# Keys and values of a second attention projected during the first attention instead of inside the second

## The chip, the core and the metric

The kernel runs on one core of a Trainium2 chip. The metric is the time of one execution on the device in microseconds. The core's engines work side by side, each through a queue of its own and in order: TensorE (PE, matrix products; its weight loads are shown apart as PEld), VectorE (DVE), ScalarE (ACT), GpSimd (POOL) and SyncE (SP, which here only issues DMA transfers). They wait for each other through semaphores. PE writes its products to PSUM, in banks that DVE or ACT empty; POOL works on SBUF alone.

## The reference

Two decoder layers run over 16 batches of 128 tokens with 256 features. With all that does not bear on the change left out, the reference is:

```python
x = x + tanh(g_xattn[0]) * L0_xattn(layernorm(x), ctx, ...)   # self- and cross-attention
x = x + tanh(g_ffn[0])   * L0_ffn(layernorm(x), ...)          # gated feed-forward
x = x + tanh(g_xattn[1]) * L1_xattn(layernorm(x), ctx, ctx, mask, ...)
x = x + tanh(g_ffn[1])   * L1_ffn(layernorm(x), ...)          # 8 experts, one per token

# L1_xattn: 32 query heads in 8 groups of 4, head size 8, causal and padded
q = (Q @ w_q.T).reshape(B, S, G, HG, HD)
k = (K @ w_k.T).reshape(B, S, G, HD)      # K = V = ctx
v = (V @ w_v.T).reshape(B, S, G, HD)
scores = einsum('bnghd,bmgd->bnghm', q, k) / sqrt(HD)
attn = softmax(where(causal & not_padded, scores, -inf))
out = einsum('bnghm,bmgd->bnghd', attn, v).reshape(B, S, D) @ w_o.T + b_o
```

The keys and values of the second attention (L1_xattn) depend on the context `ctx` and two weight matrices alone. They do not depend on `x`, so they can be computed at any time.

## The kernel before

The kernel has four stages. **The first attention** is a loop over 32 units of four steps each: units 0 to 15 are self-attention, one batch each, and units 16 to 31 cross-attention, one batch each. One loop index `n` (lines 651 to 690) drives a pipeline in which at every step different units are at different stages: `do(n, lag, name)` runs a stage for the unit and quarter that are `lag` steps behind. A step holds a score product (L503), maximum and exponentials, transposes of the probabilities (L539), the value product (L549), the output product (L590), and for a later unit two projections of 512 columns (L422), their eviction by ACT (L434) and the transposes of the normalized heads (L485, evicted by ACT at L494). The output product of a unit's last eight heads needs `cat`, which POOL writes at the end of a quantizing chain (L237). Projections go through two PSUM banks with the tag `mm`. A self-attention unit's residual is stored to DRAM (`x1`, L609) and its scaled input too (`xqx`, L400), all on SP's queue, as are the loads of `xb` (L587), of `ctx` for the cross units (L346, a tag with two buffers) and of the weights.

**The feed-forward** follows (L721 to L757), group by group of four batches.

**The second attention** is a loop of 64 steps, four to a batch (L1132 to L1160), over four groups of four batches. For a group, `front_step` loads the context transposed (`cT`, 512 KB, issued by POOL at L933) and the mask, normalizes `x`, transposes it, and projects queries and keys (`qk`, two column blocks each, L982, evicted by ACT at L987 and L989). The key weights come in with every group's eight columns repeated four times, once for each query head of the group, so a key projection has 256 columns. For a batch, `keys` makes `kb` on POOL, the keys masked by head (L1000), projects the values (L1006) and has DVE copy them four times into a zero-padded tile `vpad` (L1011). A step then does mask (L1022) and score products (L1029), the maximum on DVE, exponentials on ACT (L1045), transposes (L1056), DVE copies (L1057), and every second step the value products (L1072). A batch's output product is at L1085. The first group's front runs inside the feed-forward, at `g == 1`.

**The experts** close the kernel; they read rows that POOL scattered to DRAM (L870).

Functions issue their instructions in the order of the source, but the build may put a queue in another order: it places an instruction when its inputs and its buffer are free, and prefers the one that is earlier in the source.

Of the kernel before, what the change touches and what calls it, by code (L numbers as in the profile page):

```python
# [9 lines left out]
F32 = mybir.dt.float32  # L10
# [4 lines left out]
AF = mybir.ActivationFunctionType  # L15
# [3 lines left out]
P = 128  # L19
B = 16  # L20
DM = 256
KD = DM // P
# [13 lines left out]
def flamingo_kernel(  # L36
# [27 lines left out]
    nc = tc.nc  # L64
# [4 lines left out]
    NH, NG, HD = 32, 8, 8  # L69
# [4 lines left out]
    psum = psum0.enter_context(tc.tile_pool(name="psum", bufs=2, space=bass.MemoryType.PSUM))  # L74
    dram = ctx.enter_context(tc.tile_pool(name="dram", bufs=1, space=bass.MemoryType.DRAM))
# [4 lines left out]
    def ps_mm(shape):  # L80
        return ps("mm", shape, 2)
# [30 lines left out]
    def kpn(ap):  # L112
        return ap.rearrange("(k p) n -> p k n", p=P)
# [129 lines left out]

    xqx = dram.tile([B, P, KD * P], F32, name="xqx")
    x1 = dram.tile([B, P, DM], F32, name="x1")
    NU = 2 * B


# [2 lines left out]
    with (  # L251
# [359 lines left out]
        units = [Unit(u) for u in range(NU)]  # L611


        loads = {}

        def at(n, f, *args):
# [151 lines left out]
    SCALE1 = 1.0 / math.sqrt(HD)  # L768
    NQ = NH // NG
# [9 lines left out]
    for j in range(B):  # L779
# [9 lines left out]
        out=before, in_=ones, pattern=[[1, P]], compare_op=ALU.is_gt, fill=0.0,  # L789
# [20 lines left out]
    def route(b0, G):  # L810
# [73 lines left out]
    cq = f1.enter_context(tc.tile_pool(name="a1c", bufs=1, side="right", reuse_waits="tile"))  # L884
    gp = f1.enter_context(tc.tile_pool(name="a1f", bufs=2, side="right", reuse_waits="tile"))
    aq = cq.tile([P, KD, DM], F32, name="aq")
    ak = cq.tile([P, KD, DM], F32, name="ak")
    av = cq.tile([P, KD, NG * HD], F32, name="av")
    ao = cq.tile([P, KD, DM], F32, name="ao")
    bo = cq.tile([P, DM], F32, name="bo")  # L890
    nc.sync.dma_start(out=aq, in_=kpn(aqT))
    nc.sync.dma_start(out=ak, in_=kpn(akT))
    nc.sync.dma_start(out=av, in_=kpn(avT))
    nc.sync.dma_start(out=ao, in_=kpn(aoT))
    nc.sync.dma_start(out=bo, in_=b_o.partition_broadcast(P))

# [6 lines left out]
        out=causal, in_=causal, pattern=[[-1, P]], compare_op=ALU.is_ge, fill=NEG,  # L903
# [5 lines left out]
    for q in range(P // 32):  # L909
        rows = hmask[32 * q : 32 * q + 32, :]  # L910
        nc.gpsimd.memset(rows, 1.0)
        nc.gpsimd.affine_select(
            out=rows, in_=rows, pattern=[[-HD, NQ]], compare_op=ALU.is_ge, fill=0.0,
# [3 lines left out]
            out=rows, in_=rows, pattern=[[HD, NQ]], compare_op=ALU.is_ge, fill=0.0,  # L917
# [4 lines left out]
    vpads = [cq.tile([P, NG, NQ, 32], F32, name=f"vpad{i}") for i in range(2)]  # L922
# [6 lines left out]
    front = {}  # L929

    def load(g):
        cT = gp.tile([P, KD, NT], F32, tag="cT", name="cT")
        nc.gpsimd.dma_start(out=cT, in_=kpn(ctxT)[:, :, g * NT : (g + 1) * NT])  # L933
        mi = gp.tile([P, NT], I32, tag="mi", name="mi", bufs=1)
        nc.sync.dma_start(
            out=mi, in_=mask[g * NT : (g + 1) * NT].partition_broadcast(P)
        )
        comb = gp.tile([P, G, P], BF16, tag="comb", name="comb")
        pad = gp.tile([P, NT], F32, tag="pad", name="pad", bufs=1)
        nc.vector.tensor_scalar(pad, mi, 0.0, NEG, ALU.is_equal, ALU.mult)  # L940
# [4 lines left out]
        front[g] = {"cT": cT, "comb": comb}  # L945

    def norm(g):
        rows = [x[b] for b in range(g * G, (g + 1) * G)]
# [22 lines left out]
            nc.scalar.copy(hT[:, k, :], pt.rearrange("p n t -> p (n t)"))  # L971
        front[g]["hT"] = hT

    def qk(g, i, c):

        f = front[g]
        if c == 0:
            f[i] = gp.tile([P, KD, NT], F32, tag="qk"[i], name="qk"[i] + "T")
        w, src = ((aq, f["hT"]), (ak, f["cT"]))[i]
        pm = psum.tile([P, NT], F32, tag="mm", name="ps_mm")  # L980
        for k in range(KD):
            nc.tensor.matmul(  # L982
                pm, w[:, k, c * P : (c + 1) * P], src[:, k, :],
                start=(k == 0), stop=(k == KD - 1),
            )
        if i == 0:
            nc.scalar.activation(f[i][:, c, :], pm, AF.Copy, scale=SCALE1)  # L987
        else:
            nc.scalar.copy(f[i][:, c, :], pm)  # L989

    kbs, vps, es, eTs, oTs, scs, mxs = {}, {}, {}, {}, {}, {}, {}

    def keys(b):

        g, j = divmod(b, G)
        f = front[g]
        tok = slice(j * P, (j + 1) * P)
        kb = ap.tile([P, KD, NQ, P], F32, tag="kb", name="kb")
        for c in range(KD):
            nc.gpsimd.tensor_tensor(  # L1000
                kb[:, c], f[1][:, c, None, tok].to_broadcast([P, NQ, P]),
                hmask[:, :, None].to_broadcast([P, NQ, P]), ALU.mult,
            )
        pm = psum.tile([P, NG, HD], F32, tag="mm", name="ps_mm")
        for k in range(KD):
            nc.tensor.matmul(  # L1006
                pm, f["cT"][:, k, tok], av[:, k, :], start=(k == 0), stop=(k == KD - 1)
            )
# [3 lines left out]
        kbs[b], vps[b] = kb, vp  # L1012

    def scores(n):

        b, c, p = n // 4, n // 2 % 2, n % 2
        g, j = divmod(b, G)
        f = front[g]
        tok = slice(j * P, (j + 1) * P)
        s = psum.tile([P, 2, NQ, P], F32, tag="sc", name="ps_sc", bufs=2)  # L1020
        for i in range(2):
            nc.tensor.matmul(  # L1022
                s[:, i], identb, f["comb"][:, j, None, :].to_broadcast([P, NQ, P]),
                start=True, stop=False,
            )
        with tc.high_priority(offset=100):
            for i in range(2):
                rows = slice(32 * (2 * p + i), 32 * (2 * p + i) + 32)
                nc.tensor.matmul(  # L1029
                    s[:, i], f[0][rows, c, tok], kbs[b][rows, c], start=False, stop=True  # L1030
                )
        scs[n] = s

# [64 lines left out]
    def front_step(g, i):  # L1098

        if i == 0:  # L1100
            load(g)
            norm(g)
        elif i == 3:
            turn(g)
        elif 5 <= i < 9:
            qk(g, (i - 5) // 2, (i - 5) % 2)

    hds = {}
    for g in range(B // G):
# [3 lines left out]
        for b in range(g * G, (g + 1) * G):  # L1113
# [18 lines left out]
    for n in range(-2, N1 + 5):  # L1132
# [17 lines left out]
        g, i = divmod(n + 12, 16)  # L1150
# [10 lines left out]
    for stages in routes:  # L1161
        for _ in stages:
# [13 lines left out]
    for e in range(NE):  # L1176
# [6 lines left out]
            out=xe, in_=disp[e * CAP : (e + 1) * CAP, :].rearrange("(c p) d -> p c d", p=P)  # L1183
# [14 lines left out]
        for c in range(NCC):  # L1198
            po = ps_sc([P, DM])
            for f in range(NFC):  # L1200
# [9 lines left out]
                out=out_rows,  # L1210
# [81 lines left out]
```

## Time and profile before

| what | time |
|---|---|
| three runs, median (lowest to highest) | 1516.2 us (1514.5 to 1518.29) |
| the profiled execution, its own time | 1515.79 us |
| its span | 1514.1 us |
| PE busy | 1381.9 us (91% of the span) |
| PE weight loads busy | 1004.0 us (66%) |
| DVE busy | 1022.1 us (68%) |
| ACT busy | 810.6 us (54%) |
| POOL busy | 672.7 us (44%) |
| TensorE clock granted, mean | 0.974 of full |

Times of the profile are microseconds from the start of the span, unless marked ns. A line such as `L1006 PE MATMUL ps_mm<-av,cT 128*128 128x64 f32 x4` names the source line, the engine, the operation, the tile written and the tiles read, the shape, and how many such records follow each other. A float32 product of this kernel leaves two records, so x4 are two matmul instructions. A bracket gives the idle time before a group and what ended it. Ends of matmuls are modelled, starts are recorded.

### The profile page before, as it was taken

The numbers are of one execution on the slowest core, as the hardware profiler recorded it, in microseconds if no ns is written. First come the engines' busy times: TensorE is split into PE (matmuls) and PEld (weight loads), VectorE is DVE, ScalarE is ACT, GpSimd is POOL, SyncE is SP. The second block draws the span as 40 slices with busy tenths as digits, with TensorE's granted clock in tenths as the row PEclk, the third lists the DMA queues.
The fourth block names the chain that finished last, engine by engine and source line by source line (L and its number), as shares of the span: only waits on it lengthen the run. The fifth ranks groups of instructions, "written<-read, shape, count | busy, mean of one in ns | idle before, by whom it ended". The sixth has DMA issues, their size and how long they took to land. (4 is left out here: it accounts for less than half of the span.)

```text
span 1514.1 us, 24690 instructions
## 1 busy us (share of the span) xinstructions
PE 1381.9 (91%) x8612; PEld 1004.0 (66%) x8612; DVE 1022.1 (68%) x2756; ACT 810.6 (54%) x2421; POOL 672.7 (44%) x574
## 2 busy tenths in 40 slices
PE   2789899898988999999999987999999999996998
PEld 1477677677766777777777764555556565654887
DVE  8988878786887876767777664533678787882100
ACT  3666666666666766666666651543445454542121
POOL 4577676777667455565655553120121311111111
PEclk9799999999999999999999998999999999996999
DMA  4301001000031100000000006200300100012662
GB/s 120 118 8 32 15 15 32 11 19 15 22 91 50 49 26 11 18 15 18 15 15 19 5 8 194 61 0 0 112 22 8 50 9 36 9 40 66 202 195 64
DMA packets 51116, 68.69 MB, mean 45 GB/s; under 512 B 5291, under 2 KB 37739, under 8 KB 50992
## 3 DMA queue, kind: packets, MB, share of 16 engines
q1 hardware_dynamic: 36912, 41.31, 9.0%
q10 hardware_dynamic: 11456, 17.63, 3.6%
q0 software_dynamic: 2624, 8.16, 1.5%
q8 instruction: 69, 1.13, 0.3%
q14 instruction: 55, 0.45, 0.1%
HBM read 50.53 MB, written 16.81 MB: 44 GB/s over the span
## 5 line engine op out<-in xcount | busy, mean ns | idle before, releaser
L531 POOL TENSOR_TENSOR e<-e,sums 128x512 f32<-128x512 f32 x128 | 139.7, 1091 | 226.7 <-DVE sums L527 108.8
L474 POOL TENSOR_TENSOR raw<-raw,q_r 128x512 f32<-128x512 f32 x192 | 211.9, 1129 | 19.8 <-DVE q_r L464 18.9
L519 ACT ACTIVATE e<-ps_sc,mx 128x128 f32<-128x128 f32 x512 | 181.4, 369 | 65.0 <-DVE mx L511 56.5
L443 DVE BATCH_NORM_STATS2 q_st<-raw 128x6 f32<-128x128 f32 x768 | 174.0, 278 | 61.7 <-ACT raw L434 61.3
L1045 ACT ACTIVATE e<-ps_sc,mx 128x128 f32<-128x128 f32 x512 | 139.7, 383 | 117.5 <-DVE mx L1036 106.4
L590 PE MATMUL ps_acc<-wp,cat 128*128 128x512 f32 x512 | 159.4, 433 | 27.4 <-POOL cat L237 26.9
L237 POOL TENSOR_TENSOR cat<-e_t,e_e 128x1024 fp32r<-128x1024 bf16 x64 | 136.3, 2129 | 47.4 <-DVE e_t L231 47.4
L541 ACT COPY eT<-ps_tr 128x512 f32<-128x512 f32 x128 | 75.4, 589 | 151.7 <-PE ps_tr L539 151.6
L503 PE MATMUL ps_sc<-kT,qT 128*128 128x128 f32 x1024 | 140.4, 280 | 17.1 <-ACT qT L494 17.1
L503 PEld LDWEIGHTS ps_sc<-kT,qT 128*128 128x128 f32 x1024 | 131.0, 193 | 35.4 <-ACT qT L494 28.7
L1000 POOL TENSOR_TENSOR kb<-kT,hmask 128x512 f32<-128x512 f32 x32 | 33.6, 1068 | 243.8 <-PE ps_sc L1029 184.5
L590 PEld LDWEIGHTS ps_acc<-wp,cat 128*128 128x128 f32 x512 | 94.7, 191 | 69.6 <-POOL cat L237 35.9
L549 PE MATMUL ps_pv<-eT,vt 128*128 128x256 f32 x512 | 132.8, 381 | 1.0 <-DVE cat_y L560 1.0
L485 PE MATMUL ps_tr<-ident,raw 128*128 128x128 f32 x768 | 115.4, 277 | 16.1 <-POOL raw L474 14.2
L434 ACT COPY raw<-ps_mm 128x512 f32<-128x512 f32 x192 | 114.0, 594 | 26.6 <-PE ps_mm L422 24.1
L485 PEld LDWEIGHTS ps_tr<-ident,raw 128*128 128x128 f32 x768 | 91.9, 142 | 50.4 <-POOL raw L474 23.5
L549 PEld LDWEIGHTS ps_pv<-eT,vt 128*128 128x128 f32 x512 | 96.5, 190 | 31.5 <-issue 11.4
L560 DVE TENSOR_TENSOR cat_y<-ps_pv,r_sm 128x512 bf16<-128x512 f32 x128 | 86.9, 679 | 39.9 <-PE ps_pv L549 39.7
L511 DVE TENSOR_REDUCE mx<-ps_sc 128x4 f32<-128x512 f32 x128 | 87.1, 680 | 36.5 <-PE ps_sc L503 35.9
L494 ACT ACTIVATE qT<-ps_tr,hv 128x512 f32<-128x512 f32 x128 | 101.1, 790 | 17.5 <-PE ps_tr L485 15.5
L519 ACT ACTIVATION_READ_ACCUMULATOR e<-ps_sc,mx 128x1 f32 x512 | 105.7, 206 | 0.0
L1036 DVE TENSOR_REDUCE mx<-ps_sc 128x8 f32<-128x1024 f32 x64 | 78.1, 1221 | 25.6 <-PE ps_sc L1029 23.5
(227 smaller groups left out, 2769.0 us busy)
## 6 DMA issues: line engine op xcount, KB each, us to landing
w1t<-in_w ACTq DMA_DIRECT2D x8, 1024.0 KB, 5.1
w2t<-in_w ACTq DMA_DIRECT2D x8, 1024.0 KB, 5.5
disp<-empty SPq DMA_DIRECT2D x16, 257.0 KB, 8.3
xe<-disp SPq DMA_DIRECT2D x8, 514.0 KB, 3.6
stage<-in_wprojT SPq DMA_DIRECT2D x16, 256.0 KB, 2.8
xg<-in_x SPq DMA_DIRECT2D x4, 512.0 KB, 3.9
xb<-in_x SPq DMA_DIRECT2D x16, 128.0 KB, 2.0
ctx<-in_ctxT SPq DMA_DIRECT2D x16, 128.0 KB, 2.2
```

The costliest lines, as they stand in the source:

```text
L237: ins = nc.gpsimd.tensor_tensor(dst, t[:, part], e[:, part], ALU.subtract)
L434: nc.scalar.copy(raw.rearrange("p h d -> p (h d)"), pm)
L443: nc.vector.bn_stats(self.st[:, 4 * blk + j, :], self.raws[blk][:, j, :])
L474: ins = nc.gpsimd.tensor_tensor(src, src, self.r[:, 4 * blk : 4 * blk + 4, None].to_broadcast([P, 4, P]), ALU.mult,)
L485: nc.tensor.transpose(pt[:, j, :], src[:, j, :], ident)
L494: nc.scalar.activation(dst, pt, AF.Identity, scale=hv[:, col : col + 1], bias=hv[:, col + 1 : col + 2])
L503: nc.tensor.matmul(pscore[:, j, :], qT[:, j, :], self.kT[:, 2 * c + j // 2, :], start=True, stop=True,)
L519: nc.scalar.activation(e[:, j, :], pscore[:, j, :], AF.Exp, bias=self.mx[:, j : j + 1], accum_out=sums[:, j : j + 1],)
L531: nc.gpsimd.tensor_tensor(e, e, sums[:, :, None].to_broadcast([P, 4, P]), ALU.mult)
L549: nc.tensor.matmul(pv[:, 2 * g : 2 * g + 2, :], self.vt[:, gg * P : (gg + 1) * P], eT[:, 2 * g : 2 * g + 2, :], start=True, stop=True,)
L590: nc.tensor.matmul(self.acc, self.cat[c // 2][:, h % 8, :], wpr[self.cross, c][:, j, :, :], start=(h == 0), stop=(h == 15),)
L1045: nc.scalar.activation(e[:, i, :], s[:, i // NQ, i % NQ, :], AF.Exp, bias=mx[:, i : i + 1])
```

## The change

The keys and values of the second attention are computed during the first attention's self-attention units, one batch at a time, and kept in two DRAM tensors, `k1s` (64 rows, one for each group and feature, by all tokens) and `v1s` (tokens by 64). In step `n = 4b + 3` batch `b` is projected, for `b` up to 14, and batch 15 at `n = 61`; the call stands between the step's second projection and its output product. Each takes two matmuls for the keys, two for the values, two ACT copies and two stores on SP. The batch's context is loaded four steps ahead, into the tag `ctx` that the cross units use. The key weights are loaded without the fourfold repetition.

The second attention loses its key projections, value projections, the load of `cT`, and two weight loads. It loads instead, on SP, for each group the keys by 16 transfers of eight partitions (each repeats a group's keys for the query heads) and the values by one. The padded values are now written by one POOL copy per batch in place of four DVE copies.

```diff
@@ first attention @@
+    k1s = dram.tile([NG * HD, B * P], F32, name="k1s")
+    v1s = dram.tile([B * P, NG * HD], F32, name="v1s")
...
+        ak = ap.tile([P, KD, NG * HD], F32, tag="ak", name="ak", bufs=1)
+        av = ap.tile([P, KD, NG * HD], F32, tag="av", name="av", bufs=1)
+        cxs = {}
+
+        kv1_at = {4 * b + 3: b for b in range(B - 1)}
+        kv1_at[4 * (B - 1) + 1] = B - 1
+
+        def load_kv1(b):
+            if b == 0:
+                for k in range(KD):
+                    nc.sync.dma_start(
+                        out=ak[:, k].rearrange("p (g d) -> p g d", d=HD),
+                        in_=akT[k * P : (k + 1) * P, :].rearrange(
+                            "p (g h d) -> p g h d", h=NH // NG, d=HD
+                        )[:, :, 0, :],
+                    )
+                nc.sync.dma_start(out=av, in_=kpn(avT))
+            cxs[b] = ap.tile([P, KD, P], F32, tag="ctx", name="ctx")
+            nc.sync.dma_start(out=cxs[b], in_=kpn(ctxT)[:, :, b * P : (b + 1) * P])
+
+        def kv1(b):
+            cx = cxs.pop(b)
+            tok = slice(b * P, (b + 1) * P)
+            pm = ps_mm([P, P + NG * HD])
+            for k in range(KD):
+                nc.tensor.matmul(
+                    pm[: NG * HD, :P], ak[:, k, :], cx[:, k, :], start=(k == 0), stop=(k == KD - 1)
+                )
+            for k in range(KD):
+                nc.tensor.matmul(
+                    pm[:, P:], cx[:, k, :], av[:, k, :], start=(k == 0), stop=(k == KD - 1)
+                )
+            ko = ap.tile([NG * HD, P], F32, tag="ko", name="ko")
+            vo = ap.tile([P, NG * HD], F32, tag="vo", name="vo")
+            nc.scalar.copy(ko, pm[: NG * HD, :P])
+            nc.scalar.copy(vo, pm[:, P:])
+            nc.sync.dma_start(out=k1s[:, tok], in_=ko)
+            nc.sync.dma_start(out=v1s[tok, :], in_=vo)
...
                 ab[1][0].bn(ab[1][1])
+            if n + 4 in kv1_at:
+                load_kv1(kv1_at[n + 4])
+            if n in kv1_at:
+                kv1(kv1_at[n])
             do(n, 5, "output")
@@ second attention @@
-    ak = cq.tile([P, KD, DM], F32, name="ak")
-    av = cq.tile([P, KD, NG * HD], F32, name="av")
...
-    nc.sync.dma_start(out=ak, in_=kpn(akT))
-    nc.sync.dma_start(out=av, in_=kpn(avT))
...
     def load(g):
-        cT = gp.tile([P, KD, NT], F32, tag="cT", name="cT")
-        nc.gpsimd.dma_start(out=cT, in_=kpn(ctxT)[:, :, g * NT : (g + 1) * NT])
+        tok = slice(g * NT, (g + 1) * NT)
+        kT = gp.tile([P, KD, NT], F32, tag="k", name="kT")
+        for r in range(0, P, HD):
+            q = r // 32
+            nc.sync.dma_start(
+                out=kT[r : r + HD],
+                in_=k1s.rearrange("(c q d) t -> q d c t", q=4, d=HD)[q][:, :, tok],
+            )
+        v = gp.tile([P, G, NG * HD], F32, tag="v", name="v")
+        nc.sync.dma_start(out=v, in_=v1s[tok, :].rearrange("(b t) n -> t b n", t=P))
...
-        vp = vpads[b % 2]
-        for i in range(NQ):
-            nc.vector.tensor_copy(vp[:, :, i, HD * i : HD * i + HD], pm)
+        vp = vpads[b % 2][:]
+        nc.gpsimd.tensor_copy(
+            bass.AP(vp.tensor, vp.offset, [vp.ap[0], [P, NG], [32 + HD, NQ], [1, HD]]),
+            f["v"][:, j, :].rearrange("p (g d) -> p g d", d=HD)[:, :, None, :].to_broadcast(
+                [P, NG, NQ, HD]
+            ),
+        )
```

The rest of the diff drops the two key calls and the value matmuls: `qk(g, i, c)` becomes `queries(g, c)`, and `front_step` calls it at two places in place of four.

More of the change, by code (lines that the diff above doesn't have):

```diff
@@ L944, in load @@
         )
-        front[g] = {"cT": cT, "comb": comb}
+        front[g] = {"k": kT, "v": v, "comb": comb}
     def norm(g):
@@ L972, in turn, with queries @@
         front[g]["hT"] = hT
-    def qk(g, i, c):
+    def queries(g, c):
         f = front[g]
         if c == 0:
-            f[i] = gp.tile([P, KD, NT], F32, tag="qk"[i], name="qk"[i] + "T")
-        w, src = ((aq, f["hT"]), (ak, f["cT"]))[i]
+            f["q"] = gp.tile([P, KD, NT], F32, tag="q", name="qT")
         pm = psum.tile([P, NT], F32, tag="mm", name="ps_mm")
@@ L982, in qk @@
             nc.tensor.matmul(
-                pm, w[:, k, c * P : (c + 1) * P], src[:, k, :],
+                pm, aq[:, k, c * P : (c + 1) * P], f["hT"][:, k, :],
                 start=(k == 0), stop=(k == KD - 1),
             )
[L986 to L989, printed above, removed]
+        nc.scalar.activation(f["q"][:, c, :], pm, AF.Copy, scale=SCALE1)
     kbs, vps, es, eTs, oTs, scs, mxs = {}, {}, {}, {}, {}, {}, {}
@@ L1000, in keys @@
             nc.gpsimd.tensor_tensor(
-                kb[:, c], f[1][:, c, None, tok].to_broadcast([P, NQ, P]),
+                kb[:, c], f["k"][:, c, None, tok].to_broadcast([P, NQ, P]),
                 hmask[:, :, None].to_broadcast([P, NQ, P]), ALU.mult,
             )
[L1004 to L1008, printed above, removed]
-        vp = vpads[b % 2]
-        for i in range(NQ):
-            nc.vector.tensor_copy(vp[:, :, i, HD * i : HD * i + HD], pm)
-        kbs[b], vps[b] = kb, vp
+        vp = vpads[b % 2][:]
[5 more added lines that the diff above has]
+        )
+        kbs[b], vps[b] = kb, vpads[b % 2]
     def scores(n):
@@ L1029, in scores @@
                 nc.tensor.matmul(
-                    s[:, i], f[0][rows, c, tok], kbs[b][rows, c], start=False, stop=True
+                    s[:, i], f["q"][rows, c, tok], kbs[b][rows, c], start=False, stop=True
                 )
@@ L1104, in front_step @@
             turn(g)
-        elif 5 <= i < 9:
-            qk(g, (i - 5) // 2, (i - 5) % 2)
+        elif 5 <= i < 7:
+            queries(g, i - 5)
     hds = {}
```

## The prediction

> **What bounds the kernel now.** I read the busy shares first, then the same shares by stage, then the PE queue in order of time inside the two attentions. The cuts at 60, 430, 450, 910, 1055 and 1365 us separate start, self-attention, hand-over, cross-attention, feed-forward, second attention and experts. Columns: length, then busy time of PE, weight loads, DVE, ACT and POOL, then the granted clock.
>
> ```profile
> 60.00:430.00 370.00, 328.07 (x1892) 273.25 (x1893) 294.39 (x886) 236.91 (x743) 262.74 (x211) 0.99 0.08 24
> 450.00:910.00 460.00, 443.04 (x2312) 330.67 (x2310) 334.00 (x931) 298.57 (x913) 270.41 (x212) 1.00 0.07 22
> 1055.00:1365.00 310.00, 306.89 (x3273) 189.31 (x3271) 243.61 (x516) 157.40 (x551) 53.21 (x50) 0.99 0.10 35
> ```
>
> PE is nearly always busy in the second attention (306.9 of 310 us), but leaves 42 us of 370 open in self-attention. "Busy" is soft because ends of matmuls are modelled, so I use starts only. PE's queue in the second attention (start, duration, line):
>
> ```profile
> 1187.72 1.09 PE L1056 MATMUL ps_tr<-ident,e 128*128 128x128 f32 x8
> 1188.65 0.56 PE L1006 MATMUL ps_mm<-av,cT 128*128 128x64 f32 x4
> 1189.05 0.59 PE L1022 MATMUL ps_sc<-comb,identb 128*128 128x512 bf16 x2
> 1189.57 1.13 PE L1029 MATMUL ps_sc<-kb,qT 32*128 32x512 f32 x4
> ...
> 1194.41 1.06 PE L1072 MATMUL ps_pv<-eT,ones 128*32 128x128 f32 x32
> 1195.40 1.98 PE L982 MATMUL ps_mm<-cT,ak 128*128 128x512 f32 x4
> 1197.22 0.59 PE L1022 MATMUL ps_sc<-comb,identb 128*128 128x512 bf16 x2
> ```
>
> No bracket names a wait: each group starts when the one before has had its slot. Over 1050 to 1370 us the score groups (L1029) start 1.06 us ahead of the next group and the mask groups (L1022) 0.53 us, at the median, with few exceptions. So **PE's slots are the time here**, and a slot taken out should move all behind it. A V projection (L1006) has a slot of 1189.05 - 1188.65 = 0.40 us, half a K projection (L982, one column block of one group) 1197.22 - 1195.40 = 1.82 us.
>
> In self-attention it is different. At each unit's end:
>
> ```profile
> 320.63 1.18 PE L422 MATMUL ps_mm<-wk,xs 128*128 128x512 f32 x4
> 321.64 0.60 PE L485 MATMUL ps_tr<-ident,raw 128*128 128x128 f32 x4
> 323.31 1.20 PE L590 MATMUL ps_acc<-wp,cat 128*128 128x512 f32 x4 [1.06 <-POOL cat L237]
> ```
>
> Four transposes elsewhere have a slot of 0.36 us; here the output product starts 1.67 us after them, because POOL's last quantizing step (2.13 us) ends only then. That leaves PE 1.3 us empty, and the same gap stands ahead of 13 of the 16 units' output products (0.8 to 2.2 us, mostly 1.30). The new projections stand directly before that product in the program.
>
> **What the change removes.** K: 4 groups x 2 column blocks x 1.82 us = 14.6 us of PE slots, of which group 0's two (3.60 us, seen at 996.40) lie in the feed-forward, where PE also runs without a gap, and six (10.9 us) in the second attention. V: 16 x 0.40 = 6.4 us. Sum **20.9 us**, 17.3 of it in the second attention. Also gone: 8 ACT copies (586 ns) and 64 DVE copies (213 ns), 4.7 and 13.6 us by duration, which I cost at nothing: ACT is busy 157 and DVE 244 of 310 us there, both less than PE. The POOL-issued ctx loads (0.77 us x4) and one 8.9 us wait of POOL behind them go too; PE waited for neither.
>
> What is late next there? Per step (64 in 310 us, 4.84 us each) DVE needs 3.8 us, and after the change PE still needs 4.57. The cover shrinks, and in steps without a projection PE's own need (0.53 + 1.06 + 0.93 + 0.95 = 3.5 us) is near DVE's. I give back 1 us for that, bounds 0 and 3.
>
> A rule speaks against so much. The Trainium skill ("Trainium Kernel Development and Optimization", Performance Expectations) calls matmul busy time a bad measure and weight-load busy time a good one. That is 189.3 of 310 us here, 61%; read so, PE has slack and 17.3 us of slots would return some 10.6 us (estimate from that page and the row). The starts say otherwise: they follow each other at fixed distances with no wait. I take the whole 17.3, and let the range hold the other.
>
> **What it adds on PE.** Per batch two 128-column K matmuls and two 64-column V matmuls. The V pair is the pair removed: 0.40 us. The K pair has 64 stationary columns, not in the trace; nearest is the score product L503, where four matmuls of 128 columns have a slot of 0.89 us, so two take 0.45 (below it: the V pair's 0.40, which has half the moving columns). 0.85 us x16 = **13.6 us**. If all 13 gaps of about 1.3 us take one, 3 x 0.85 = 2.6 us stay exposed; if the projections are issued elsewhere, up to 13.6. I take 2.6, by the row of the gap.
>
> The order is not certain. Queues are not in source order: an instruction goes ahead once its inputs and buffer are free. Cross unit 16 and 17's ctx loads, placed near loop step 56, are issued before 6 us:
>
> ```profile
> 4.79 0.94 SPq L346 DMA_DIRECT2D ctx<-in_ctxT  x2
> ```
>
> So the early batches may be projected in the first 60 us, where PE is busy only 24.5 us; that hides them as well, but puts waits at the head of queues.
>
> **ACT.** Two small copies per batch; nearest are 0.37 us (128x128 from PSUM) and 0.19 (128x24), so 0.4 to 0.75 us, 16 times, at most 12 us on an engine with 133 us free in self-attention. Right after the shown gap ACT is idle (next work 324.98, idle 1.87 us). Behind the copies wait only the next step's eT copy and exponentials. One of the two ps_mm banks is held until they are done; successive projections start 2 to 3 us apart with evictions ending about 1.8 us after a start, so the spare bank is short but there. I put 2 us for ACT, banks and the start together, bounds 0 and 8.
>
> **DMA and SP.** Self-attention gets 3 weight loads, 16 ctx loads and 32 stores on SP, about 0.35 us each to issue; there SP now issues three per unit and mostly stands waiting, so its time is free, not its order. The strided weight load (32-byte runs) is nearest to wgt, which has the same runs and landed in 1.7 us; it may have 26 us and more.
>
> For each group the second attention gets 16 loads of 32 KB and one of 128 KB. The Trainium skill ("DMA: Bandwidth & Descriptors", Rules for kernel authors) says to coalesce: under 64 KB one pays mostly overhead. One after the other at the 2.0 us an xb load takes, a group would need 32 us; by the rows, issue 0.33 us x16 and one landing of 1.7 us, 7 us. They are placed ten steps, 48 us, ahead of their use, and group 0's have from 948 us (bo issued) to 999 (first kb). Both prices fit, so 0; if SP stood blocked for over 16 us in front of them, the first would show.
>
> **POOL.** 16 pad copies of 256 elements, not in the trace: half of a kb multiply (1.07 us) is 0.53, a 128x256 ln_y 1.25; 8 to 20 us on an engine busy 53 of 310. I take 0.6 us each, and 0 for the time. Each inherits the wait for the values product of two batches ago. Behind it on POOL stand the next kb, ln_y and the row scatters; those waits are longer today (kb: 184 us on the scores) without PE naming them, and the copy is needed some six steps later.
>
> **Sum**, against the profiled execution (1515.8 us, span 1514.1): 1515.8 - 20.9 + 2.6 + 1 + 2 = 1500.5, rounded to **1500**; the median of the runs, 1516.2, lies 0.4 higher, inside the rounding. The bounds: all hidden, 1495; 13.6 us exposed and 3 + 8 lost, 1519.
>
> **Rivals.** (a) *Given back* (chance 0.13): the projections land where PE has no gap. 13.6 us exposed plus 1 and 2: 1511.5, about no change. For it: the free order above. Against: the gap is right where they stand.
>
> (b) *Slower* (0.12): SP's order. The ctx load of a later batch waits for the buffer of an earlier one, then stands in SP's queue behind an x1 store that waits for DVE, 223 us over 12 times, up to 20.6 us (the SP queue's own waits, below), while the projection is already at the head of PE's queue and everything behind it waits too.
>
> ```profile
> SPq L609 <- DVE lnT L368: 223.2, 12, 20.6
> ```
>
> The point is 18 us lost beyond my 2.6, 1.1 us per batch; at 2.5 us each for 15 batches 37.5 us are lost, and the time is 1500 + 37 = 1537. Against: in program order a ctx load has a whole unit of lead (26 us, from the gap at 297.6 to the one at 323.3), so it needs projections pulled forward to the load's own landing.
>
> (c) *All hidden* (0.05): start and gaps take every projection, the second attention gives all: 1494.
>
> **How the numbers follow.** The forecast (1495 to 1509) has 0.70. Measurement tells 0.3%, 4.5 us, from no change: faster below 1511.6. From the forecast and (c) 0.75, and half of (a), 0.06, are faster: 0.81; the other half same, 0.07; (b) slower, 0.12. Range 1494 to 1512, which leaves out (b) and some of (a).
>
> **What would show it.** Right: second attention about 17 us shorter with PE still gapless, L982 with only the query weights, no L1006; feed-forward 3.6 us shorter; the output products' wait for POOL's cat shrunk from 1.06 to a few tenths with kv1's matmuls before it, self-attention within 5 us. Wrong: PE or PE's weight loads waiting for a ctx DMA or ACT's small copies; kv1's matmuls away from the gap; PE idle in the second attention waiting for DVE, for kb or the pad.

## The result, and the profile after

| | before | after |
|---|---|---|
| median (lowest to highest), 6 runs of each | 1516.27 us (1514.50 to 1518.85) | 1511.13 us (1508.84 to 1511.87) |
| ratio after / before, 95% interval | | 0.9962 (0.9948 to 0.9975) |
| profiled execution, its span | 1515.8, 1514.1 us | 1511.0, 1509.2 us |

The change makes the kernel 5.1 us faster, by the medians. The forecast was 16. To see where the rest went I cut both profiled executions at six marks that a reader can find by name: the fourth group of transposes of `xh` and the last one (the self-attention units lie between them), the first product with `wgu`, the first and last mask product of the second attention, and the end. Differences are taken before rounding.

| stretch | before | after | difference |
|---|---|---|---|
| start, to the fourth group | 115.4 us | 118.2 us | +2.7 |
| self-attention units, to the last group | 292.5 | 301.6 | +9.1 |
| rest of the first attention | 524.4 | 531.0 | +6.6 |
| feed-forward | 123.2 | 119.6 | -3.6 |
| second attention | 298.8 | 279.7 | -19.2 |
| rest | 159.7 | 159.2 | -0.4 |

The gains came, in the places named. The first attention gave back 18.4 us of them. First the busy shares by stage of the kernel after, in the columns that were used before (length, then PE, weight loads, DVE, ACT, POOL, clock):

```profile
60.00:430.00 370.00, 332.45 (x1945) 276.70 (x1946) 291.50 (x858) 233.86 (x744) 253.36 (x202) 0.99 0.09 28
450.00:910.00 460.00, 443.31 (x2295) 330.65 (x2293) 338.79 (x946) 296.31 (x895) 270.36 (x212) 0.99 0.09 26
1055.00:1365.00 310.00, 304.90 (x3240) 184.48 (x3239) 243.29 (x470) 160.23 (x556) 56.75 (x62) 1.00 0.11 36
```

PE is busy for only 4.4 us more in the 370 us of self-attention, though 13 projections of about 1.1 us have gone in there, and stays idle for 37.5 us. Fewer units fit into the same stretch now, so this row alone does not tell what the 9.1 us are; the waits below do. Now PE's queue in the second attention of the kernel after:

```profile
1188.84 1.06 PE L1118 MATMUL ps_pv<-eT,ones 128*32 128x128 f32 x32
1189.82 1.98 PE L1032 MATMUL ps_mm<-hT,aq 128*128 128x512 f32 x4
1191.64 0.59 PE L1068 MATMUL ps_sc<-comb,identb 128*128 128x512 bf16 x2
1192.17 1.13 PE L1075 MATMUL ps_sc<-kb,qT 32*128 32x512 f32 x4
```

Queries are projected as before (slot 1191.64 - 1189.82 = 1.82 us), there is no key or value projection, and still no bracket: the queue has moved up.

Not all of the 19.2 us is the change's. In the second attention of the kernel before, the granted clock fell to half twice, for 3.4 us each time:

```profile
1170.50:1173.90 3.40, 3.40 (x60) 2.88 (x62) 2.15 (x7) 1.35 (x6) 0.00 (x0) 0.51 0.00 0
1320.70:1324.10 3.40, 3.40 (x36) 2.99 (x39) 1.67 (x4) 2.02 (x8) 0.67 (x1) 0.50 0.00 0
```

```profile
1172.72 1.65 PE L1072 MATMUL ps_pv<-eT,ones 128*32 128x128 f32 x32
```

The same group of products took 1.06 us at 1194.41, in the prediction's rows. In the profiled execution of the kernel after, no such stretch lies in this stage. The profiles of all fourteen kernels (those of the experiments below included), sorted by the number of these stretches in their second attention, give its length in us:

| half-clock stretches | keys and values computed there | loaded |
|---|---|---|
| 0 | | 279.7, 279.9, 279.9 |
| 1 | 297.3 | 280.3, 281.6, 281.8 |
| 2 | 298.7, 298.8, 298.8 | 282.6, 282.9 |
| 3 | | 284.0, 284.7 |

At an equal number of stretches the change takes **about 16.1 us** off this stage; the other 3 us are the two stretches. Why the clock falls where it does is not shown.

Then the unit's end in self-attention, PE of the kernel after:

```profile
331.26 0.60 PE L488 MATMUL ps_tr<-ident,raw 128*128 128x128 f32 x4
331.79 0.65 PE L642 MATMUL ps_mm<-ctx,ak 128*64 128x128 f32 x4
332.37 0.66 PE L646 MATMUL ps_mm<-av,ctx 128*128 128x64 f32 x4
332.91 1.20 PE L593 MATMUL ps_acc<-wp,cat 128*128 128x512 f32 x4
333.95 1.05 PE L506 MATMUL ps_sc<-kT,qT 128*128 128x128 f32 x8
334.84 0.60 PE L542 MATMUL ps_tr<-ident,e 128*128 128x128 f32 x4
```

The projection (L642, L646) lies exactly in the gap: 1.65 us from the transposes to the output product, against 1.67 before. So do those of batches 1 to 13. Batch 0 (at 79.6 us) and batches 14 and 15 (at 471.8 and 492.5, among the cross units) found no gap. But read two lines further, and compare with what followed the output product at 323.31 in the kernel before:

```profile
324.35 0.60 PE L539 MATMUL ps_tr<-ident,e 128*128 128x128 f32 x4
324.78 1.06 PE L503 MATMUL ps_sc<-kT,qT 128*128 128x128 f32 x8
```

**Scores and probability transposes have changed places.** Nothing in the source of that step asks for it. What PE waited for between 60 and 430 us, after and then before (total, times, longest):

```profile
PE ps_sc L506 <- ACT qT L497: 19.0, 13, 2.2
PE ps_acc L593 <- POOL cat L237: 2.5, 3, 1.5
```

```profile
PE ps_acc L590 <- POOL cat L237: 14.7, 13, 2.0
PE ps_sc L503 <- ACT qT L494: 12.7, 14, 1.9
```

The wait for `cat` went from 14.7 to 2.5 us, as forecast. The wait for `qT` grew from 12.7 to 19.0. A steady unit takes 26.46 to 26.48 us, against 25.73 to 25.75: **0.74 us more in a steady unit**, and one wait for `qT` in it holds it all. After, then before:

```profile
352.78 1.16 PE L506 MATMUL ps_sc<-kT,qT 128*128 128x128 f32 x8 [1.44 <-ACT qT L497]
```

```profile
342.44 1.16 PE L503 MATMUL ps_sc<-kT,qT 128*128 128x128 f32 x8 [0.69 <-ACT qT L494]
```

The cause is on DVE. Its queue from the same point of the unit, after (output product at 332.91) and before (at 323.31):

```profile
337.27 0.69 DVE L563 TENSOR_TENSOR cat_y<-ps_pv,r_sm 128x512 bf16<-128x512 f32 x1 [1.54 <-PE ps_pv L552]
337.98 0.87 DVE L446 BATCH_NORM_STATS2 q_st<-raw 128x6 f32<-128x128 f32 x4
338.77 0.41 DVE L225 TENSOR_SCALAR cat_y<-cat_y 128x1024 bf16<-128x1024 bf16 x1
339.09 0.17 DVE L530 RECIPROCAL sums<-sums 128x4 f32<-128x4 f32 x1
...
339.83 1.06 DVE L230 TENSOR_SCALAR e_e<-e_e 128x1024 bf16<-128x1024 bf16 x1
```

```profile
327.67 0.69 DVE L560 TENSOR_TENSOR cat_y<-ps_pv,r_sm 128x512 bf16<-128x512 f32 x1 [1.10 <-PE ps_pv L549]
328.28 0.17 DVE L527 RECIPROCAL sums<-sums 128x4 f32<-128x4 f32 x1
328.40 0.43 DVE L225 TENSOR_SCALAR cat_y<-cat_y 128x1024 bf16<-128x1024 bf16 x1
328.74 0.86 DVE L443 BATCH_NORM_STATS2 q_st<-raw 128x6 f32<-128x128 f32 x4
...
330.13 0.41 DVE L230 TENSOR_SCALAR e_e<-e_e 128x1024 bf16<-128x1024 bf16 x1
```

`cat_y` comes 4.36 us after the output product in both. Before, the reciprocal of the softmax sums is next, and the four statistics of block 2 (0.86 us) stand behind the clamp. After, the statistics are first and the reciprocal last: it comes 6.18 us after the output product in place of 4.97. Between 110 and 425 us this is the order of all twelve units after, and the other that of all twelve before (the expectation of `bfirst`, below, counts 10 of 13). POOL waits for that reciprocal to divide the exponentials, before and after:

```profile
328.59 1.13 POOL L531 TENSOR_TENSOR e<-e,sums 128x512 f32<-128x512 f32 x1 [1.34 <-DVE sums L527]
331.41 2.14 POOL L237 TENSOR_TENSOR cat<-e_t,e_e 128x1024 fp32r<-128x1024 bf16 x1 [1.69 <-DVE e_t L231]
```

```profile
339.43 1.17 POOL L534 TENSOR_TENSOR e<-e,sums 128x512 f32<-128x512 f32 x1 [2.58 <-ACT raw L437]
341.76 2.14 POOL L237 TENSOR_TENSOR cat<-e_t,e_e 128x1024 fp32r<-128x1024 bf16 x1 [1.15 <-DVE e_t L231]
```

(The row after names an ACT copy, which ended 0.03 us later than the reciprocal and whose `raw` the divide does not read. The divide starts 0.17 us behind the reciprocal's end, as others do.) After, the divide starts 6.52 us behind the output product instead of 5.28, and so lies beside DVE's L230, which then takes 1.06 us and not 0.41. That is 0.65 of the 0.75 us by which `cat` starts later (8.85 us behind the output product, 8.10 before).

From `cat` to the `qT` that PE waits for it is 10.20 us after and 10.21 before, by this way: POOL writes `in_y`, the input of a later unit, DVE rounds it, and POOL writes `xs` from it. DVE's `q_dif`, a step of 24 columns that reads nothing of this, stands beside `xs` and ends 0.06 us behind it, in each unit of both kernels. Soon behind it `q_var` releases ACT's `q_a`, and `qT` is next in ACT's queue. After:

```profile
348.86 1.66 POOL L237 TENSOR_TENSOR xs<-e_t,e_e 128x768 fp32r<-128x768 bf16 x1 [0.63 <-DVE e_t L231]
349.31 1.27 DVE L453 TENSOR_TENSOR q_dif<-q_st 128x24 f32<-128x24 f32 x1
351.83 0.22 ACT L463 ACTIVATE q_a<-q_var 128x24 f32<-128x24 f32 x1 [0.85 <-DVE q_var L458]
351.96 0.76 ACT L497 ACTIVATE qT<-ps_tr,hv 128x512 f32<-128x512 f32 x1
```

The unit is **paced by this chain through DVE, POOL and ACT**. PE's gap was its slack.

### The profile page after: what moved, and what is told of

The parts are those of the page before. It is cut to its first block, busy times and chain, and to the rows that moved or that the text cites. A ratio compares the mean times of both kernels' runs of the same rounds, so it can differ in the third digit from the quotient of the medians.

```text
span 1509.2 us, 24921 instructions
## 1 busy us (share of the span) xinstructions
PE 1376.0 (91%) x8644; PEld 1001.6 (66%) x8644; DVE 1029.5 (68%) x2692; ACT 811.4 (54%) x2445; POOL 677.3 (45%) x586
## 5 line engine op out<-in xcount | busy, mean ns | idle before, releaser
L593 PE MATMUL ps_acc<-wp,cat 128*128 128x512 f32 x512 | 160.5, 436 | 18.1 <-POOL cat L237 17.3
L497 ACT ACTIVATE qT<-ps_tr,hv 128x512 f32<-128x512 f32 x128 | 101.2, 790 | 18.4 <-PE ps_tr L488 16.3
L1102 PEld LDWEIGHTS ps_tr<-ident,e 128*128 128x128 f32 x512 | 57.5, 140 | 57.8 <-ACT e L1091 21.8
```

The costliest lines, as they stand in the source:

```text
L497: nc.scalar.activation(dst, pt, AF.Identity, scale=hv[:, col : col + 1], bias=hv[:, col + 1 : col + 2])
L593: nc.tensor.matmul(self.acc, self.cat[c // 2][:, h % 8, :], wpr[self.cross, c][:, j, :, :], start=(h == 0), stop=(h == 15),)
```

## The experiments

All times are medians, and "period" is that of a steady self-attention unit. The kernels ran in several groups, each with the kernel before beside them (1515.6 to 1518.1 us), so each ratio is to the kernel before of its own group, and kernels are compared by their ratios. Differences in the last four columns are the kernel's one profiled execution less that of before, in us: start, units, rest of the first attention, second attention.

| kernel | time, us | ratio (95%) | period, us | start | units | rest | second |
|---|---|---|---|---|---|---|---|
| after | 1511.13 | 0.9962 (0.9948 to 0.9975) | 26.47 | +2.7 | +9.1 | +6.6 | -19.2 |
| kvonly | 1533.64 | 1.0099 (1.0082 to 1.0116) | 26.49 | +3.2 | +9.3 | +6.0 | -1.5 |
| bnlate | 1507.93 | 0.9929 (0.9912 to 0.9945) | 25.92 | +2.9 | +2.8 | +8.4 | -18.9 |
| bfirst | 1549.77 | 1.0210 (1.0193 to 1.0227) | 28.3 to 28.8 | +1.9 | +25.8 | +3.7 | -0.2 |
| upfront | 1510.24 | 0.9962 (0.9950 to 0.9974) | 25.73 | +13.9 | -0.1 | +3.8 | -14.1 |
| pfirst | 1500.67 | 0.9895 (0.9870 to 0.9919) | 25.75 | +3.7 | -1.2 | +3.6 | -18.5 |
| double_p | 1515.46 | 1.0004 (0.9992 to 1.0017) | 26.81 | +1.9 | +10.6 | +8.6 | -16.3 |
| owntag | 1510.89 | 0.9972 (0.9962 to 0.9981) | 26.49 | +3.2 | +9.4 | +8.8 | -14.9 |
| ends_p | 1504.92 | 0.9924 (0.9907 to 0.9940) | 25.75 | +7.2 | -1.7 | +6.4 | -17.1 |
| hand1 | 1503.94 | 0.9916 (0.9884 to 0.9947) | 25.75 | +3.5 | -1.2 | +6.3 | -18.9 |
| late1 | 1500.60 | 0.9900 (0.9868 to 0.9932) | 25.74 | 0.0 | -1.7 | +8.6 | -17.2 |
| bhand | 1521.05 | 1.0024 (1.0013 to 1.0035) | 25.75 | +0.3 | +0.1 | +6.6 | 0.0 |
| late2 | 1502.60 | 0.9895 (0.9879 to 0.9912) | 25.74 | +0.5 | -1.6 | +8.3 | -16.0 |

The profiled executions of `upfront` and `owntag` took 7 to 8 us longer than the medians of those kernels; theirs are the two with three half-clock stretches in the second attention. Differences of a few us in a column can come from such stretches, and are read below only where the clock allows it.

**The added half alone** (`kvonly`): keys and values are projected in the units and stored as in the change, and the second attention is that of before, so they are computed twice.

```diff
 second attention
-    (keys and values loaded from k1s and v1s)
+    (the load of cT, the key and value projections and the DVE copies of before)
```

> Only the added half: projections and stores as in the changed kernel, but the second attention computes its keys and values itself as before, so the stored ones are unused. Both theories: first attention 18.6 us longer, as in the changed kernel, the rest as before: about 1535. If the second attention's gain were partly owed to the first attention's state, another sum.

It took 1533.64 us and showed the same 26.49 us units as the change, and a first attention that was as much longer. So the loss belongs to the added half and the gain to the removed half. By the ratios the removed half is worth 1.0099 - 0.9962 = 1.37%, some 21 us; the forecast had 20.9 less 1.

**The order of DVE, from both sides.** `bfirst` is the kernel before with the statistics of block 2 put ahead of the clamp and the reciprocal. `bnlate` is the kernel after with them called one step later, behind the next reciprocal.

```diff
 bfirst (kernel before)
+        if ahead and len(dsts) == 1:
+            stay_after(ins, ahead[-1])        # ins: the clamp
...
+                if blk == 2 and not self.cross:
+                    ahead.append(self.bni)
...
+                if ahead:
+                    stay_after(ins, ahead.pop())   # ins: the reciprocal
```

> The kernel before with nothing of the change, but on DVE the four statistics of a self-attention unit's block 2 are held ahead of the quantizing clamp and of the softmax reciprocal, the order that the changed kernel has (10 of 13 units; the other three have it already). Theory A (the queue order costs 0.75 us a unit): 7.5 us slower than before, about 1524, all of it between 110 and 450 us, with the output products still waiting for cat. Theory B (the new projections themselves cost the time, by PE slots or PSUM banks): within 2 us of before, 1516.

```diff
 bnlate (kernel after)
+            if held:
+                u, blk = held.pop()
+                u.bn(blk)
...
+            late = bool(ab[0]) and ab[0][1] == 2 and not ab[0][0].cross
-            if ab[0]:
+            if ab[0] and not late:
...
+            if late:
+                held.append(ab[0])
```

> The changed kernel with those statistics issued behind the next step's reciprocal in self-attention units, so that clamp and reciprocal come first again in 10 of 13 units; the projections stay in the gap. Theory A: 7.5 us faster than the changed kernel, about 1503.5, unit period 25.7 us where it is 26.46 now. Theory B: same as the changed kernel, 1511, unit period 26.46.

Both moved in the direction of the theory. `bnlate` brought the period to 25.92 us with PE's order and all projections as they were, and 6.3 of the 9.1 us came back. `bfirst` slowed the kernel before without a projection in it, but it missed its forecast by far: 2.6 to 3.1 us a unit and not 0.75, 1549.77 us and not 1524. Forcing one pair changed further places of DVE's order too. So the order by itself costs time; how much the one swap costs is read from `bnlate` and the next kernel, not from `bfirst`.

**PE's order alone** (`pfirst`). In the first step of each self-attention unit the source calls the transposes ahead of the scores, which is the order that the build had chosen before. DVE's order is not touched.

```diff
-            do(n, 0, "scores")
-            do(n, 2, "probs")
+            if n % 4 == 0 and 0 < n < 4 * B:
+                do(n, 2, "probs")
+                do(n, 0, "scores")
+            else:
+                do(n, 0, "scores")
+                do(n, 2, "probs")
```

> The changed kernel with one difference: at a self-attention unit's first step the transposes of the probabilities are called ahead of the score product, the order that the kernel before had on PE after the output product. Nothing is done to DVE's statistics. Theory A (the projection in the gap makes the build swap these two on PE, that turns DVE's order, and that costs 0.75 us a unit): DVE's order goes back by itself, unit period 25.7 to 25.9 us, total some 8 us below the changed kernel, about 1503. Rival (the PE swap is harmless, or the DVE order has another cause): same as the changed kernel, 1511, period 26.46.

It took 1500.67 us, and units 25.75. Its DVE queue and PE's waits from 60 to 430 us:

```profile
330.13 0.69 DVE L563 TENSOR_TENSOR cat_y<-ps_pv,r_sm 128x512 bf16<-128x512 f32 x1 [1.11 <-PE ps_pv L552]
330.74 0.17 DVE L530 RECIPROCAL sums<-sums 128x4 f32<-128x4 f32 x1
330.86 0.43 DVE L225 TENSOR_SCALAR cat_y<-cat_y 128x1024 bf16<-128x1024 bf16 x1
331.20 0.86 DVE L446 BATCH_NORM_STATS2 q_st<-raw 128x6 f32<-128x128 f32 x4
```

```profile
PE ps_sc L506 <- ACT qT L497: 12.6, 14, 1.4
...
PE ps_acc L593 <- POOL cat L237: 1.5, 1, 1.5
```

The order of before has come back by itself, the wait for `qT` is the old one (12.6 us), and the wait for `cat` stays gone. The projections cost nothing in the units: the period is that of before, and 291.3 us against 292.5 is no gain, since the clock fell to half once in the units of before (at 184.1 us) and never in those of `pfirst`. This version beats both kernels, by 1.05% against before. `bhand` (below) has this reordering, and one more, without the change; its units are as before, so the reordering gains nothing there by itself.

**How much the gap holds** (`double_p`): `pfirst` with each projection's four matmuls issued twice into the same tile; the outcome is unchanged.

```diff
+            (the four matmuls of kv1 once more, behind the first four)
```

> That kernel with every projection's four matmuls issued twice into the same bank (the second time overwrites the first with the same values), some 1.05 us more PE time a batch; copies and stores stay single. If one projection fits the 1.3 us gap and PE's time is hidden only up to the gap: the second one is exposed, 13 to 14 us slower, about 1517, period 26.8 us. If the unit's pace is set by the POOL and DVE chain with PE slack beyond the gap: less than half of that.

```profile
330.35 0.65 PE L642 MATMUL ps_mm<-ctx,ak 128*64 128x128 f32 x4
330.93 0.66 PE L646 MATMUL ps_mm<-av,ctx 128*128 128x64 f32 x4
331.52 0.65 PE L650 MATMUL ps_mm<-ctx,ak 128*64 128x128 f32 x4
332.10 0.66 PE L654 MATMUL ps_mm<-av,ctx 128*128 128x64 f32 x4
332.56 1.19 PE L593 MATMUL ps_acc<-wp,cat 128*128 128x512 f32 x4
```

The second set costs its whole time, 26.81 - 25.75 = 1.06 us a unit. The gap takes one projection and not a second. This is what rival (a) of the prediction would look like.

**No projection in the units** (`upfront`): two batches in each of the eight loop steps ahead of the first unit.

```diff
-        kv1_at = {4 * b + 3: b for b in range(B - 1)}
-        kv1_at[4 * (B - 1) + 1] = B - 1
+        kv1_at = {}
...
+            if -8 <= n < 0:
+                for b in range(2 * (n + 8), 2 * (n + 8) + 2):
+                    load_kv1(b)
+                    kv1(b)
```

> The changed kernel with all 16 projections called in the first eight loop steps (two batches a step) instead of one in each unit. The DVE order of the units is that of before again. Theory A: units as before (25.7 us), second attention and feed-forward shorter by 23 us as in the changed kernel, and a start longer by 2 to 6 us: 1495 to 1499. Theory B (13 to 16 us wherever they stand): about 1510.

Units are those of before (25.73 us), with PE's order of before. But the start grew by 13.9 us, not by 2 to 6, and the time was 1510.24. I had taken the start for nearly free because PE is idle there. In its first 80 us PE now waits for the batches' contexts, eight times and 20.5 us in all (8.4 of them at the very start, when it has nothing else to do):

```profile
PE ps_mm L641 <- DMA ctx<-in_ctxT: 20.5, 8, 8.4
```

The projections stand at the head of PE's queue while their loads are under way, and the attention's first product with `wk` starts at 35.21 us; before, it started at 26.83. An idle engine is not a free queue. How the rest of the 13.9 us comes about was not followed.

**The rest of the first attention and the start.** `owntag` gives the early batches their own pair of context buffers.

```diff
-            cxs[b] = ap.tile([P, KD, P], F32, tag="ctx", name="ctx")
+            cxs[b] = ap.tile([P, KD, P], F32, tag="cx1", name="cx1")
```

> The changed kernel with the batches' context in two buffers of its own, so that the cross units' first contexts are loaded in the start as before. If the 4.3 us longer way from the last self-attention unit to the first cross projection come from the shared buffers: 4 us faster, 1507. If they come from the queue orders there (ACT, POOL): same, 1511.

Time and units are those of after, and this way is 46.20 us long (46.81 in after): the shared buffers are not the cause. `ends_p` is `pfirst` with batches 0, 1, 14 and 15 in the start.

```diff
+        kv1_at = {4 * b + 3: b for b in range(2, B - 2)}
+        early = {-9: 0, -8: 1, -7: 14, -6: 15}
...
+            if n in early:
+                load_kv1(early[n])
+                kv1(early[n])
```

> The transposes-first kernel with batches 0, 1, 14 and 15 projected in the start (loop steps -9 to -6) and the twelve others in the gaps. Theory A: the 2.8 us of the first units and the 4.3 us of the hand-over go, four projections in the start cost 1 us each (16 cost 15 there): 3 us below the transposes-first kernel, about 1500. If the start costs more, about the same as it.

It was no better than `pfirst`, and by the medians 4 us slower: the start grew by a further 3.5 us, and the stretch from the last unit to the first cross projection stayed (46.56 us; 46.80 in `pfirst`, 42.54 before). One wait stands out in this stretch in `pfirst`, on ACT's queue:

```profile
437.70 0.72 ACT L202 ACTIVATE wq<-stage,wsc 128x512 fp32r<-128x512 f32 x1 [4.87 <-POOL stage L214]
```

The splitting of a cross query weight stands ahead of an eviction and of exponentials there; PE then waits 3.83 us for `qT` (1.96 at this place before). The kernel after has an equally long stretch without this wait, so the expectation below is wrong where it finds the wait there. `hand1` loads and splits these weights one step later.

```diff
-            at(4 * B - 7 + c, load_split, K_QX, wqxT, c)
-            at(4 * B - 6 + c, load_split, K_QX, wqxT, c + 2)
+            at(4 * B - 6 + c, load_split, K_QX, wqxT, c)
+            at(4 * B - 5 + c, load_split, K_QX, wqxT, c + 2)
```

> The transposes-first kernel with the loads and splits of the cross units' query weights called one step later. In the changed kernel and all its variants but one, ACT has the first of these splits at the head of its queue, ahead of an eviction and four exponentials, and waits 4.9 us for POOL there; now it stands behind them, as in the kernel before. If that is the 4.3 us longer hand-over: 46.8 us from the last self-attention transpose to the first cross projection becomes about 42.5, total some 3 to 4 us below the transposes-first kernel, 1497. If the hand-over is long for another reason: same as it, 1500.7.

The hand-over fell to 43.59 us as meant, but the cross units took 4.3 us longer in this execution (434.7 us to their last projection, 430.4 in `pfirst`), with half-clock stretches of 6.8 us in them where `pfirst` has none. By the medians nothing was won. Two more move the batches themselves.

```diff
 late1 (hand1, own context buffers)
+        kv1_at = {4 * b + 11: b for b in range(B)}
 late2 (pfirst, own context buffers)
+        kv1_at = {4 * b + (11 if b < 11 else 31): b for b in range(B)}
```

> The previous kernel with every batch projected two units later (step 4b + 11), so that 13 batches fall on the units that have the gap and three on cross units, and with context buffers of their own. If the 3 us longer first units come from batches 0 and 1, which have no gap, they go, and three projections in the gapless cross-attention cost 0.9 us each: about equal to the previous kernel, 1497 to 1498. If a projection costs more where there is no gap: slower than it.

> The transposes-first kernel (cross query weights at their old place) with 11 batches projected in the gaps of steps 11 to 51 and the other five in steps 75 to 91, in cross-attention; own context buffers. No projection stands in the two steps before the hand-over, and ACT's queue has the weight split behind the exponentials there by itself. Theory: start as before (115.4 us at the fourth unit), units 25.75 us, hand-over 42.5 us instead of 46.8, cross-attention longer by five gapless projections, 5 x 0.85 = 4.3 us: first cross projection at 449, total about 1497, 3 to 4 us below the transposes-first kernel. If the hand-over stays at 46 us, the projection at its door is not what turns ACT's queue; if cross-attention grows by 8 us or more, a projection without a gap costs more than its slots.

With batch 0 two units later the start is that of before (115.4 and 115.9 us): the +2.7 us of the change come from batches 0 and 1. `late2` also has the hand-over of before (42.58 us), as `upfront` has (42.56), the other kernel without a projection in the last units. So the 4.3 us come with a projection there. But the cross units of `late2`, with five batches in them, took 6.9 us longer than before, and the ratio is `pfirst`'s. How much of the 6.9 us is the batches' own is open: `bhand`, with no batch at all, took 4.0 us longer there, with half-clock stretches of 6.8 us (3.4 in `late2`, none before). So three attempts at the edges won nothing over `pfirst`. `bhand`, last, is the kernel before with the edits of `pfirst` and `hand1` and nothing else.

```diff
 (kernel before, the two edits shown for pfirst and hand1)
```

> The kernel before with the two reorderings alone (transposes first, cross query weights one step later), nothing of the change. If they only take back what the change cost: same as before, 1515 to 1517. If they gain by themselves, part of the gain of the last kernels is not the change's.

It was slower than before by 0.24% (0.13 to 0.35). Its start and units are as before (+0.3 and +0.1 us). The rest of the first attention is 6.6 us longer in the profiled execution, with more half-clock stretches in it. So what `pfirst` gains over after in the units is the repair of what the change had upset. What the first reordering does alone, without the second, was not run.

## Where the prediction held and where it failed

- **Second attention.** Forecast 17.3 us of PE slots less 1 us for DVE, 16.3; measured 19.2 in the one pair of profiles, and 16.1 at equal clock. Slots did return the time. The Trainium skill's weight-load measure ("Trainium Kernel Development and Optimization", Performance Expectations), read as PE's slack, would have given 10.6 us. The page gives it as a measure of the distance to roofline, and here it did not measure what a slot is worth: weight loads were busy for 61% of the stage and PE's queue had no slack.
- **Feed-forward.** Forecast 3.6, measured 3.6.
- **Added PE work.** Forecast 0.85 us a batch; measured 0.58 for the keys and 0.47 to 0.55 for the values, about 1.1 in all. Thirteen went where I put them, into the gap ahead of the output product, and three found none, as I had assumed. In `pfirst` the thirteen cost nothing in the units.
- **DMA, SP and POOL at nothing.** Right. PE waits for none of the loads of keys and values, and a pad copy took 0.44 us on the mean, not 0.6. The price by which 16 small loads take 32 us for a group was not seen on PE's path.
- **The step that failed** is what the first attention would lose: 2.6 us of exposed slots and "2 us for ACT, banks and the start together, bounds 0 and 8", 4.6 us in all. It lost 18.4 us, and the sign "self-attention within 5 us" did not come true. The sum asked what the new instructions would occupy and whom they would make wait. It put nothing for what the build would do with the order of the instructions around them. I had even written that queues are not in source order, and used it only for where the projections would land. With the gap filled, the build placed scores ahead of transposes on PE, DVE's statistics went ahead of a reciprocal, and a chain that was the true pace of the unit got 0.74 us longer: 9.1 us over the units, shown by `pfirst` and `bnlate`. Another 2.7 us come from batches 0 and 1 in the start (shown by `late1`; by which wait, is open). Of the 6.6 us behind the units, 4.3 lie between the last unit and the first cross projection, and come with a projection in the last units (shown by `late2` and `upfront`, which have none there; the order that does it in the kernel after was not followed). The other 2.3 us lie in the cross units, where the clock was at half for 6.8 us and before never; whether the two batches there cost anything is open.
- **A warning overlooked.** I read PE's gap as a place that holds work. It also said that PE does not set the pace there, so that the pace must lie on other engines, whose order I never looked at.
- **Rivals.** The measured 1511.13 us is next to the 1511.5 of rival (a), by coincidence: its mechanism, projections exposed on PE, is what `double_p` shows and not what happened. Rival (b), SP's order, did not occur in the kernel after; `upfront` shows a form of it. Rival (c), 1494, everything hidden, is nearest to what `pfirst` shows in the units, with 1500.67 us in all.

## What to carry to other kernels

A gap on the busiest engine is both a place for more work and a sign that another chain sets the pace. Before counting the gap as free, follow that chain in order of time and ask whether filling the gap can change the order in which the build places its links. When a moved piece of work costs more than its own time, compare the instruction orders of all engines in one steady period; here putting two calls back into their old order turned 0.4% into 1.05%. And before a difference of a few us between two single profiles is explained, compare the granted clock of the stage in both.

## What the runs showed of the hardware

- A bf16 step on DVE waits out a POOL step that began before it. L230 (128x1024) never took more than 0.43 us between 60 and 430 us where POOL was idle at its start, in before, after and `pfirst`. In after, 12 of them started about 0.4 us behind the start of a POOL divide and took 1.06 us each. The one shown started at 339.83 and ended at 340.89, and the divide beside it at 339.43 + 1.17 = 340.60. Two others started only 0.05 us behind the divide's start, as two did before; they took 0.41 us, and there the divide took 1.37 us where it takes 1.04 alone. The Trainium skill ("SBUF — State Buffer", Who interferes with whom) describes the two engines' shared ports as an exclusive lock, held for a whole instruction by whichever starts first, and the trace agrees. Delaying a divide on POOL by 1.24 us thus cost 0.65 us on DVE. The float32 step `q_dif` of 24 columns shows the same: 1.03 to 1.28 us beside `xs` in 13 units of both kernels, 0.17 us the one time that POOL was idle.
- The slot of two 128-column products with 64 stationary columns was 0.58 us, more than half the 0.89 us of four with 128, which I had taken as measure.
- In a stage where PE's queue had no gap, a stretch of 3.4 us at half the clock made the stage about 1.5 us longer (298.8 us with two, 297.3 with one, for the same code). In the start it made no such difference: 115.4 us in before and 115.9 in `late2`, with 27.3 and 10.2 us of it at half clock.
